# Round three of a graph network: finishing tiles inside the loop of sums, marks by five blocks, an entry that follows the gathers by groups

## The chip, the cores and the metric

The kernel runs on one core of a Trainium2 chip, as one program. The metric is the device time of one execution in microseconds (us). A core has five engines that work side by side, each through its own list of instructions: TensorE (PE, matrix products and transposes; its weight loads are listed as PEld), VectorE (DVE), ScalarE (ACT), GpSimd (POOL, here mostly gathers by index) and SyncE (SP, which only starts transfers). An engine takes its instructions strictly in order: one that waits holds up all that stand behind it.

## The reference, cut to what matters

The network has four rounds. Each adds to the state x (3125 nodes, 256 features, f32) the result of a graph step and then that of a feed-forward step, both on the normalised state:

```
x = x + L2_gnn(layernorm(x), edge_index, edge_weight, ...)   # round three
x = x + L2_ffn(layernorm(x), ...)

def L2_gnn(h, ...):
    deg  = segment_sum(weights with loops, row);  dinv = where(deg > 0, rsqrt(deg), 0)
    norm = dinv[row] * weight * dinv[col]
    xw   = h @ W
    h7   = segment_sum(xw[col] * norm, row) + b
    return relu(h7 @ W1 + b1) @ W2 + b2

def L2_ffn(x, ...):                       # experts gated by graph attention
    h = (x @ W_gat);  a_src, a_dst = sums of h * att_src, h * att_dst
    e = leaky_relu(a_src[src] + a_dst[dst]);  softmax of e over the edges of each dst
    agg = segment_sum(softmax * h[src]);  scores -> two best of four experts -> MLPs
```

Round three's attention runs over edges of its own (65,536 and loops), which the kernel has to bring into the order of their destinations first.

## The kernel before, in words

Nodes lie in T = 25 tiles of P = 128; five tiles are a group (TG = 5). The state X stays in on-chip memory as 128 x 25 x 256. DC = 2 is the number of 128-wide pieces of the 256 features. The edges of the attention lie in 25 blocks, one for each tile, of KB = 17 columns of 128 edges (KL = 8 in the last block).

**Entry.** The experts of round two leave their results in memory (ff_results). `gated` ends with a loop over tiles, `mix_result` (L1018): two gathers by index (gb_y, L348) on POOL's queue and two additions to X on DVE (L1024) for each tile, 50 gathers in all. Round three's `r2_gnn` (L1056) normalises X (`moe_input`, `norm_group` L171: group operations on DVE, a square on ACT, `rsqrt` L153), transposes it (`transposed` L198), and multiplies it by W (r_p, L1080). The scaled result is r2_xw.

**Loop of sums.** `src_sum` (L2379) runs 27 steps. Step t loads one column of the dense graph matrix from memory (ss_wt, 1.6 MB, on SP's queue, L2402, two buffers) and adds up 25 products into ss_sum (L2405, 50 matmul instructions in the trace): the sums of tile t. Beside it, `own_order` (L1839) brings block after block of the attention's edges into order. It is a generator, cut into pieces by `yield`, and the loop takes it a piece at a time:

1. ACT: one-hot matrix oo_h of the block's destinations (17 x L1849, then L1850).
2. DVE: partial sums of it and a scan (L1858 to L1870).
3. PE: two matmuls into oo_p (L1874, L1875). DVE: from them each edge's place (L1879 to L1897, ends in oo_pf). ACT: a second one-hot matrix oo_hp from oo_pf (17 x L1849, L1850). DVE: oo_rh (L1907).
4. PE: 17 matmuls of oo_hp and oo_rh (L1912), which move the edges to their places.
5. DVE: the results are stored in own_gi and own_rel (L1915 to L1917).

A step t takes piece 1 of block t, piece 3 of block t-1, piece 4 of block t-2, the sums of tile t, piece 5 of block t-2, then `done` for tile t-1 (r_acc: two DVE operations, L1086 and L1087), and piece 2 of block t. `in_order` (L1968) makes the order of instructions on PE, DVE and ACT the order in which the program issues them here. So on PE: L1874 and L1875 of block t-1, 17 x L1912 of block t-2, sums of tile t.

**Behind the loop.** `own_marks` (L1920) and `mark_edges` (L1676) find for all 25 blocks where an edge's destination differs from its neighbour's (matmuls of om_ends with om_near, L1939), and turn this into rows of masks: 25 transposes of 4 columns (te_e into te_pr, L1696) and four of 104 columns (L1701), which SP stores as relT. Then r_acc is transposed (L205), the MLP follows in groups of four tiles (L1104, relu L1106, L1111; X += b2 and X += product on DVE, L1113 and L1114), and `r2_ffn` (L2412) begins: loads of expert weights issued by ACT (L2429 to L2433), layernorm, transposes to q_xT, products with the attention weights (100 matmuls, L2454), a copy to q_hx (ACT, L2456), its store to memory (q_rows, SP), and q_ad (DVE, L2458). `attend_blocks` then gathers rows of q_rows for every edge column (ad_rows, L348, 416 gathers on POOL).

The function that the changed kernel calls from step to step is new; of the old ones these lines carry most of the time:

```
            for k in range(kb):                                   # one_hot: ACT, pieces 1 and 3
                nc.scalar.activation(y[:, k, :], self.iotab, AF.Abs, bias=minus[:, k:k + 1])
            nc.scalar.activation(out[:, :kb, :], y[:, :kb, :], AF.Relu, scale=-1.0, bias=self.ones[:, 0:1])
```

Of the kernel before, what the change touches and what calls it, by code (L numbers as in the profile page):

```python
# [24 lines left out]
F32 = mybir.dt.float32  # L25
BF16 = mybir.dt.bfloat16
I32 = mybir.dt.int32
AF = mybir.ActivationFunctionType
OP = mybir.AluOpType
AX = mybir.AxisListType  # L30
PSUM = bass.MemoryType.PSUM
DRAM = bass.MemoryType.DRAM

P = 128
N = 3125
T = 25
NP = T * P
D = 256
DC = D // P
EPS = 1e-5  # L40
BIG = 1e30
NOWHERE = float((1 << 23) + (1 << 22))
GR = 4
TG = 5
# [5 lines left out]
KB = 17  # L50
KL = 8
# [10 lines left out]
class Net:  # L62
# [90 lines left out]
    def rsqrt(self, pool, out, v):  # L153

        nc = self.nc
        r = pool.tile(list(v.shape), F32, name="rs_r")
        h = pool.tile(list(v.shape), F32, name="rs_h")
        nc.scalar.activation(r, v, AF.Sqrt)
        nc.vector.reciprocal(r, r)
        nc.vector.tensor_mul(h, r, r)  # L160
        nc.vector.tensor_mul(h, h, v)
        nc.vector.tensor_scalar(h, h, -0.5, 1.5, op0=OP.mult, op1=OP.add)
        nc.vector.tensor_mul(out, r, h)
# [1040 lines left out]
class Fast(Net):  # L1204
# [471 lines left out]
    def mark_edges(self, s, first, pool, p2, psp):  # L1676

        nc, K = self.nc, s.K
        nc.vector.tensor_scalar(s.neg, s.rel, float(P), -BIG, op0=OP.is_ge, op1=OP.mult)

        go = pool.tile([P, K], F32, name="te_go")
        nc.vector.memset(go, 1.0)
        for k in s.k0:
            nc.vector.memset(go[:, k:k + 1], 0.0)
        st = pool.tile([P, K], F32, name="te_st")
        nc.vector.tensor_tensor_scan(st, go, first, 0.0, OP.mult, OP.max)
        nc.vector.tensor_scalar_mul(s.cum, st, -BIG)
        nc.vector.tensor_scalar(go, go, -1.0, 1.0, op0=OP.mult, op1=OP.add)
        nc.vector.tensor_max(go, go, first)
        nc.vector.tensor_scalar_mul(s.drop, go, -BIG)  # L1690
        for b in range(T):
            e = p2.tile([P, 4], F32, name="te_e")
            k = s.k0[b] + s.kb[b] - 1
            nc.vector.tensor_copy(e, s.cum[:, k:k + 1].to_broadcast([P, 4]))
            ps = psp.tile([P, P], F32, name="te_pr")[0:4, :]
            nc.tensor.transpose(ps, e, self.ident)  # L1696
            nc.vector.tensor_copy(s.dropT[:, b, :], ps)
        W = 104
        for k in range(0, K, W):
            ps = psp.tile([P, P], F32, name="te_pr")[0:W, :]  # L1700
            nc.tensor.transpose(ps, s.rel[:, k:k + W], self.ident)  # L1701
            r = p2.tile([W, P], BF16, name="te_r")
            nc.vector.tensor_copy(r, ps)
            nc.sync.dma_start(s.relT[k:k + W, :], r)
# [90 lines left out]
    def own_load(self):  # L1795
# [6 lines left out]
        self.edge_tiles(s, keep, "own", self.d.rec.rearrange("p k f -> p (k f)"))  # L1802
        s.low = keep.tile([P, KB, KB], BF16, name="own_low")
# [116 lines left out]
    def own_marks(self):  # L1920

        nc, tc, s = self.nc, self.tc, self.o
        K = s.K
        with tc.tile_pool(name="om", bufs=1) as pool, tc.tile_pool(name="om2", bufs=2) as p2, \
                tc.tile_pool(name="om_ps", bufs=2, space=PSUM) as psp:
            n = KB * (T - 1)
            ends = pool.tile([P, 2, T], F32, name="om_ends")
            full = s.rel1[:, 0:n].rearrange("p (d k) -> p d k", k=KB)
            for i, (u, v) in enumerate(((KB - 1, KL - 1), (0, 0))):
                nc.vector.tensor_copy(ends[:, i, 0:T - 1], full[:, :, u])  # L1930
                nc.vector.tensor_copy(ends[:, i, T - 1:T], s.rel1[:, n + v:n + v + 1])
            near = pool.tile([P, 2, P], F32, name="om_near")
            nc.vector.memset(near, 0.0)
            nc.vector.tensor_copy(near[:, 0, 1:P], self.ident[:, 0:P - 1])
            nc.vector.tensor_copy(near[:, 1, 0:P - 1], self.ident[:, 1:P])
            first = pool.tile([P, K], F32, name="om_first")
            ps = psp.tile([P, 2, T], F32, name="om_p")
            for i in range(2):
                nc.tensor.matmul(ps[:, i, :], near[:, i, :], ends[:, i, :], start=True, stop=True)  # L1939
            r, f, l = s.rel1, first, s.last  # L1940
            nc.vector.tensor_tensor(f[:, 1:K], r[:, 1:K], r[:, 0:K - 1], OP.not_equal)
            nc.vector.tensor_tensor(l[:, 0:K - 1], r[:, 0:K - 1], r[:, 1:K], OP.not_equal)
            nc.vector.tensor_tensor(f[:, 0:n].rearrange("p (d k) -> p d k", k=KB)[:, :, 0], full[:, :, 0], ps[:, 0, 0:T - 1], OP.not_equal)
            nc.vector.tensor_tensor(l[:, 0:n].rearrange("p (d k) -> p d k", k=KB)[:, :, KB - 1], full[:, :, KB - 1],
                                    ps[:, 1, 0:T - 1], OP.not_equal)
            nc.vector.tensor_tensor(f[:, n:n + 1], r[:, n:n + 1], ps[:, 0, T - 1:T], OP.not_equal)
            nc.vector.tensor_tensor(l[:, K - 1:K], r[:, K - 1:K], ps[:, 1, T - 1:T], OP.not_equal)
            no = pool.tile([P, K], F32, name="om_no")
            nc.vector.tensor_scalar(no, r, 0.0, 256.0, op0=OP.is_equal, op1=OP.mult)
            nc.vector.scalar_tensor_tensor(s.rel, r, -1.0, no, op0=OP.add, op1=OP.add)  # L1950
            self.mark_edges(s, first, pool, p2, psp)
# [409 lines left out]
    def r1_ffn(self):  # L2361
        with self.mix_way:
            self.gated(self.mix, "L1_ffn_w1", "L1_ffn_b1", "L1_ffn_w2", "L1_ffn_b2", AF.Gelu, send=3)
        self.own_send()
# [14 lines left out]
    def src_sum(self, rows, done):  # L2379


        nc, tc = self.nc, self.tc
        self.own_load()
        with tc.tile_pool(name="ss_w", bufs=2) as wp, tc.tile_pool(name="ss_ps", bufs=2, space=PSUM) as psp, \
                tc.tile_pool(name="oo", bufs=2) as op, tc.tile_pool(name="oo1", bufs=1) as o1, \
                tc.tile_pool(name="oo_ps", bufs=1, space=PSUM) as osp, \
                self.in_order(nc.tensor, nc.vector, nc.scalar):
            ways, sums = {}, {}

            def step(b):  # L2390
                if b in ways:
                    next(ways[b])

            for t in range(T + 2):
                if t < T:
                    ways[t] = self.own_order(t, op, o1, osp)
                step(t)
                step(t - 1)
                step(t - 2)
                if t < T:  # L2400
                    wt = wp.tile([P, T, P], F32, name="ss_wt")
                    nc.sync.dma_start(wt, self.mats[:, t, :, :])  # L2402
                    sums[t] = psp.tile([P, D], F32, name="ss_sum")
                    for d in range(T):
                        nc.tensor.matmul(sums[t], wt[:, d, :], rows[:, d, :], start=d == 0, stop=d == T - 1)  # L2405
                step(t - 2)
                if t - 1 in sums:
                    done(t - 1, sums[t - 1])
                step(t)
        self.own_marks()  # L2410

    def r2_ffn(self):  # L2412
# [7 lines left out]
        with ExitStack() as ctx:  # L2420
            pool = ctx.enter_context(tc.tile_pool(name="q", bufs=1))
# [17 lines left out]
            for e in range(1, E):  # L2439
                nc.vector.memset(early[:, e, 0:e], 1.0)  # L2440
            we = self.head_weights(pool, a["L2_ffn_W_gat"], a["L2_ffn_att_src"].rearrange("h c -> (h c)"),
                                   a["L2_ffn_att_dst"].rearrange("h c -> (h c)"), C=4)
            xT = self.moe_input(pool)
            hx = pool.tile([P, T, Q + 4], F32, name="q_hx")
            ad = pool.tile([P, T, 4], F32, name="q_ad")
            sf = pool.tile([P, T, 4], F32, name="q_sf")
            rows = self.dram.tile([NP, Q + 4], F32, name="q_rows")
            with tc.tile_pool(name="q_ps", bufs=2, space=PSUM) as psp:
                for g in range(0, T, TG):
                    gs = slice(g, g + TG)  # L2450
                    ps = psp.tile([P, TG, Q + 8], F32, name="q_hp")
                    for t in range(TG):
                        for c in range(DC):
                            nc.tensor.matmul(ps[:, t, :], xT[:, c, (g + t) * P:(g + t + 1) * P], we[:, c, :],  # L2454
                                             start=c == 0, stop=c == DC - 1)
                    nc.scalar.copy(hx[:, gs, :], ps[:, :, 0:Q + 4])  # L2456
                    nc.sync.dma_start(rows[g * P:(g + TG) * P, :].rearrange("(t p) w -> p t w", p=P), hx[:, gs, :])
                    nc.vector.tensor_copy(ad[:, gs, :], ps[:, :, Q + 4:Q + 8])  # L2458
                nc.vector.tensor_add(sf, hx[:, :, Q:Q + 4], ad)
                nc.vector.scalar_tensor_tensor(sf, sf, 0.2, sf, op0=OP.mult, op1=OP.max)  # L2460
# [156 lines left out]
```

## Time and profile before

| what | us |
|---|---|
| median of 14 runs | 5074.15 (5064.08 to 5081.76) |
| profiled execution | 5076.92 |
| its span | 5075.1 |
| result gathers of round two, first to last start | 2520.57 to 2583.79 |
| first transpose of round three's entry on PE | 2590.83 |
| first sums in the loop | 2651.94 |
| last sums end | 3011.2 |
| marks, last transpose | 3039.96 |
| transposes of r_acc, first start | 3042.24 |
| MLP, first and last start on PE | 3058.88, 3104.98 |
| layernorm's first square on ACT | 3119.53 |
| score matmuls, start | 3153.48 |

The page of the whole span gives PE 69% busy, DVE 57%, ACT 41%, POOL 41%; the mean granted clock of PE is 0.83 of its full rate. These shares are means over some ten stages with different limits, so the stage that the change touches, from 2520 to 3180, has to be read by itself: which engine is full in it, and what each engine waits for. Rows of the timeline give start, length, engine, line, operation, result and operands, shape and count, and in brackets how long the engine had been idle before and which instruction let it go on. Rows of a stretch give its length and then for each engine the busy time and the number of instructions, then the granted PE clock, the busy share of the DMA engines and GB/s. PE's rows overlap by a little, since matmuls are pipelined.

### The profile page before, as it was taken

To read this page: it belongs to the slowest core of one execution; us is meant where nothing else is said; L and a number is where in the kernel's file an instruction comes from. 1 tells how busy PE (TensorE), PEld (TensorE's weight loads), DVE (VectorE), ACT (ScalarE), POOL (GpSimd) and SP (SyncE) were. 2 spreads that over 40 slices of the span, in tenths; PEclk is the share of its full clock that TensorE was granted. 3 is DMA by queue.
4 is the path that set the end of the run, shared out by engine and by line. 5 is a ranking of instruction groups with operands and counts; after the bars stand their busy time and mean duration, and the time that the engine had idled before them with its cause. 6 is when DMAs were issued, how large, how long until landed. Compare 5 with 4: busy or idle time off the path is not lost. (4 is left out here: it accounts for less than half of the span.)

```text
span 5075.1 us, 65672 instructions
## 1 busy us (share of the span) xinstructions
PE 3490.4 (69%) x20836; PEld 2764.9 (54%) x20836; DVE 2893.3 (57%) x9538; ACT 2062.0 (41%) x5659; POOL 2094.3 (41%) x2082
## 2 busy tenths in 40 slices
PE   1399969646566254553748877057877999988993
PEld 1289958534444143342537754034544788877883
DVE  7988852356665366663358884477765874321112
ACT  3466432136666367661129972022322331112220
POOL 0686443557775777775520000777710000110003
PEclk9699979877777677776969986577887999998997
DMA  1642237544443344432723311111100112215554
GB/s 56 197 138 103 92 119 221 174 117 143 139 143 101 100 137 129 132 105 91 210 68 117 117 71 45 31 35 31 35 5 7 71 66 77 92 68 181 189 191 137
DMA packets 329438, 542.96 MB, mean 107 GB/s; under 512 B 69074, under 2 KB 242006, under 8 KB 325876
## 3 DMA queue, kind: packets, MB, share of 16 engines
q1 hardware_dynamic: 213434, 354.48, 20.7%
q0 software_dynamic: 84032, 154.27, 11.7%
q10 hardware_dynamic: 31610, 29.84, 1.7%
q8 instruction: 172, 2.82, 0.2%
q14 instruction: 190, 1.56, 0.1%
HBM read 393.49 MB, written 145.37 MB: 106 GB/s over the span
## 5 line engine op out<-in xcount | busy, mean ns | idle before, releaser
L348 POOL DMA_INDIRECT ad_rows<-r_rows,fa_gi x832 | 821.6, 988 | 285.0 <-issue 240.2
L1785 POOL DMA_INDIRECT os_table<-os_rec,os_at x512 | 555.6, 1085 | 565.2 <-ACT gx_h L994 171.5
L348 POOL DMA_INDIRECT ad_rows<-q_rows,own_gi x416 | 403.7, 970 | 718.4 <-issue 711.3
L2165 ACT ACTIVATE ad_rows<-ad_rows 128x64 f32<-128x64 f32 x2544 | 617.0, 334 | 1.6
L2175 PE MATMUL ad_acc<-ad_rows,ad_hd 128*128 128x260 f32 x1664 | 518.7, 465 | 4.0 <-ACT ad_rows L2165 2.6
L857 POOL DMA_INDIRECT regions<-gh_xn,gd_at x150 | 157.9, 1053 | 846.5 <-PE r_o L1644 625.5
L1629 PE MATMUL r_pa<-r_xs,r_cnt 128*128 128x257 bf16 x3750 | 468.1, 277 | 28.1 <-DVE r_xs L1405 14.2
L994 ACT ACTIVATE gx_h<-gx_pa,gx_bias 128x256 f32<-128x256 f32 x392 | 185.8, 474 | 586.3 <-PE gx_pa L993 562.2
L1629 PEld LDWEIGHTS <-r_cnt 128*128 128x128 bf16 x3750 | 365.3, 99 | 85.1 <-issue 29.4
L2175 PEld LDWEIGHTS ad_acc<-ad_rows,ad_hd 128*128 128x128 f32 x1664 | 367.3, 233 | 71.1 <-ACT ad_rows L2165 7.1
L2078 PE MATMUL ad_pt<-ident,ad_e 128*4 128x128 f32 x75 | 26.6, 354 | 540.1 <-DVE ad_e L2075 409.6
L965 DVE TENSOR_TENSOR gx_ys<-gx_po,gx_b 128x256 f32<-128x256 f32 x168 | 70.5, 423 | 539.0 <-PE gx_po L963 536.9
L993 PE MATMUL gx_pa<-gx_xt,gx_w 128*128 128x256 f32 x1568 | 367.1, 389 | 4.8 <-DMA gx_w<-in_L_ffn_W 3.4
L963 PE MATMUL gx_po<-gx_w,gx_h 128*128 128x256 f32 x1568 | 366.8, 380 | 0.0
L348 POOL DMA_INDIRECT gb_y<-ff_results,gd_at x150 | 151.1, 1008 | 480.7 <-SPq L120 427.9
L993 PEld LDWEIGHTS gx_pa<-gx_xt,gx_w 128*128 128x128 f32 x1568 | 294.6, 193 | 70.8 <-DVE gx_xt L988 18.7
L2078 PEld LDWEIGHTS ad_pt<-ident,ad_e 128*4 128x4 f32 x75 | 6.1, 82 | 572.6 <-issue 541.5
L963 PEld LDWEIGHTS gx_po<-gx_w,gx_h 128*128 128x128 f32 x1568 | 289.8, 190 | 38.4 <-ACT gx_h L994 2.1
L1510 PE MATMUL r_pa<-r_xn,r_wt 128*128 128x257 f32 x1250 | 300.3, 385 | 9.2 <-ACT r_wt L1545 7.9
L2405 PE MATMUL ss_sum<-r_xw,ss_wt 128*128 128x256 f32 x1250 | 293.9, 398 | 6.3 <-DMA ss_wt<-mats 6.3
L2405 PEld LDWEIGHTS ss_sum<-r_xw,ss_wt 128*128 128x128 f32 x1250 | 248.1, 200 | 43.0 <-issue 6.6
L1510 PEld LDWEIGHTS r_pa<-r_xn,r_wt 128*128 128x128 f32 x1250 | 229.9, 193 | 38.0 <-ACT r_wt L1545 8.5
(556 smaller groups left out, 6911.0 us busy)
## 6 DMA issues: line engine op xcount, KB each, us to landing
gx_w<-in_L_ffn_W SPq DMA_DIRECT2D x56, 1024.0 KB
mats<-r_wt SPq DMA_DIRECT2D x25, 1600.0 KB
ss_wt<-mats SPq DMA_DIRECT2D x25, 1600.0 KB
gx_w<-in_L_ffn_W SPq DMA_DIRECT2D x56, 512.0 KB
regions<-zero SPq DMA_DIRECT2D x26, 1024.0 KB
ad_rb<-fa_relT SPq DMA_DIRECT2D x48, 544.0 KB
gx_xs<-regions SPq DMA_DIRECT2D x84, 256.0 KB
ff_results<-gx_ys ACTq DMA_DIRECT2D x84, 256.0 KB
```

The lines of the kernel that those rows point to most:

```text
L348: return self.nc.gpsimd.indirect_dma_start(out=out, out_offset=None, in_=table[:, :], in_offset=bass.IndirectOffsetOnAxis(ap=idx, axis=0))
L857: ins = nc.gpsimd.indirect_dma_start(out=self.regions[:, :], out_offset=bass.IndirectOffsetOnAxis(ap=m.at[i][:, t:t + 1], axis=0), in_=x, ...
L963: nc.tensor.matmul(po, h[:, f, j * P:(j + 1) * P], w2s[:, f, :], start=f == 0, stop=f == FC - 1)
L965: nc.vector.tensor_add(y[:, j, :], po, b2s)
L993: nc.tensor.matmul(ps, w1s[:, c, f * P:(f + 1) * P], xt[:, c, :], start=c == 0, stop=c == DC - 1)
L994: done = nc.scalar.activation(h[:, f, :], ps, act, bias=bias1[:, f, k:k + 1])
L1510: nc.tensor.matmul(pa, wt[:, i, :], xn[:, g * G + i, :], start=i == 0, stop=i == G - 1)
L1629: nc.tensor.matmul(pa, c[:, u, :], xs[i - 1][:, u, j, :], start=u == 0 and j == 0, stop=u == T - 1 and j == 2)
L1785: i = nc.gpsimd.indirect_dma_start(out=s.table[:, :], out_offset=bass.IndirectOffsetOnAxis(ap=s.at[:, c:c + 1], axis=0), in_=s.rec[:, c, : ...
L2165: i = nc.scalar.activation(v, v, AF.Copy, scale=x.rt[:, k, W4 + h:W4 + h + 1])
L2175: nc.tensor.matmul(x.acc, lhs[:, k, :], rhs[:, k, :], start=i == 0, stop=i == x.kb - 1)
L2405: nc.tensor.matmul(sums[t], wt[:, d, :], rows[:, d, :], start=d == 0, stop=d == T - 1)
```

## The change

It rewrites `r2_gnn` and takes `src_sum` into it; the parts that moved out of `r2_ffn` are gone there.

- **Entry.** The tail of `gated` is left out (`tail=False`); `r2_gnn` itself goes over the five groups: the ten gathers and additions of a group, its layernorm, its transposes (copies all on ACT), its products with W. The 25 additions of b2 to X stand on POOL, issued after the loop of groups; in POOL's own order 15 of them lie between gathers, the first after the 23rd gather, and 10 behind the last.
- **Finish.** `finish(t, total)` is a generator of four pieces for one tile: r_acc's two operations (here lt_acc); transposes (pt) and a copy on ACT; the first product (ph) and two relus on ACT; the second product (po) and the addition to X on DVE. The first is taken at the end of step t+1, the others by `on()`, one in each later step.
- **Scores.** When the last tile of a group is finished, `scores(g)` is added: layernorm of the group, transposes, copies to q_xT, products, store of q_rows, one piece a step, in nine pieces.
- **Marks.** `own_marks` takes five blocks, in two pieces, after the blocks 4, 9, 14, 19 and 24.
- **Order.** `on()` stands behind piece 4 of block t-2 and ahead of the sums of tile t. It takes one piece of everything in the list `later`. After step 26 the rest is taken by repeated `on()`.
- **Buffers.** pt, ph and the score transposes share lt_pt, two buffers of PSUM; po and the score products share lt_po, one buffer; the marks' matmul and transposes share te_pr, one buffer.

```diff
+            near = pool.tile([P, 2, P], F32, name="om_near")
...
+                for g in range(0, T, TG):
+
+                    for t in range(g, g + TG):
+                        self.mix_result(self.mix, bp, t)
+                    xn = xp.tile([P, TG, D], F32, name="r2_xn")
+                    self.norm_group(lp, xn, g)
...
+                for t in range(T):
+                    nc.gpsimd.tensor_add(self.X[:, t, :], self.X[:, t, :], b2)
...
+                    tc.tile_pool(name="om_ps", bufs=1, space=PSUM) as mps, \
...
+                    tc.tile_pool(name="lt_ps", bufs=2, space=PSUM) as bank, \
+                    tc.tile_pool(name="lt_po", bufs=1, space=PSUM) as one, \
+                    self.in_order(nc.tensor, nc.vector, nc.scalar):
...
+                def finish(t, total):
+
+                    acc = tp.tile([P, D], F32, name="lt_acc")
+                    nc.vector.tensor_add(acc, total, xw[:, t, :])
+                    nc.vector.scalar_tensor_tensor(acc, acc, dv[:, t:t + 1], b, op0=OP.mult, op1=OP.add)
+                    yield
+                    pt = bank.tile([P, 512], F32, name="lt_pt")[:, 0:DC * P].rearrange("p (c n) -> p c n", c=DC)
+                    for c in range(DC):
+                        nc.tensor.transpose(pt[:, c, :], acc[:, c * P:(c + 1) * P], self.ident)
+                    at = tp.tile([P, DC, P], F32, name="lt_at")
+                    nc.scalar.copy(at, pt)
+                    yield
+                    ph = bank.tile([P, 512], F32, name="lt_pt")[:, 0:DC * P].rearrange("p (c n) -> p c n", c=DC)
...
+                    for f in range(DC):
+                        nc.scalar.activation(h[:, f, :], ph[:, f, :], AF.Relu, bias=b1[:, f:f + 1])
+                    yield
+                    po = one.tile([P, D], F32, name="lt_po")
+                    for f in range(DC):
+                        nc.tensor.matmul(po, h[:, f, :], w2[:, f, :], start=f == 0, stop=f == DC - 1)
+                    nc.vector.tensor_add(self.X[:, t, :], self.X[:, t, :], po)
+                    if t % TG == TG - 1:
+                        later.append(scores(t + 1 - TG))
...
+                    for u, v in ((0, 2), (2, 4), (4, 5)):
+                        pt = bank.tile([P, 512], F32, name="lt_pt").rearrange("p (c t n) -> p c t n", t=2, c=DC)
...
+                        nc.scalar.copy(q.xT[:, :, (g + u) * P:(g + v) * P].rearrange("p c (t n) -> p c t n", n=P), pt[:, :, 0:v - u, :])
+                        yield
+                    ps = one.tile([P, D], F32, name="lt_po")[:, 0:TG * (Q + 8)].rearrange("p (t w) -> p t w", t=TG)
...
+                    nc.scalar.copy(q.hx[:, gs, :], ps[:, :, 0:Q + 4])
+                    nc.sync.dma_start(q.rows[g * P:(g + TG) * P, :].rearrange("(t p) w -> p t w", p=P), q.hx[:, gs, :])
+                    nc.vector.tensor_copy(q.ad[:, gs, :], ps[:, :, Q + 4:Q + 8])
...
+                def on():
+                    for way in later[:]:
+                        if next(way, StopIteration) is StopIteration:
+                            later.remove(way)
+
                 for t in range(T + 2):
                     if t < T:
                         ways[t] = self.own_order(t, op, o1, osp)
                     step(t)
                     step(t - 1)
                     step(t - 2)
+                    on()
                     if t < T:
                         wt = wp.tile([P, T, P], F32, name="ss_wt")
                         nc.sync.dma_start(wt, self.mats[:, t, :, :])
                         sums[t] = psp.tile([P, D], F32, name="ss_sum")
                         for d in range(T):
+                            nc.tensor.matmul(sums[t], wt[:, d, :], xw[:, d, :], start=d == 0, stop=d == T - 1)
                     step(t - 2)
                     if t - 1 in sums:
-                        done(t - 1, sums[t - 1])
+                        way = finish(t - 1, sums[t - 1])
+                        next(way)
+                        later.append(way)
                     step(t)
+                    if t >= 2 and (t - 2) % TG == TG - 1:
+                        later.append(self.own_marks(mp, mp2, mps, near, t - 1 - TG, t - 1))
+                while later:
+                    on()
```

## The prediction

> **What bounds it now.** First the page's chain that ended last, then busy time by stretch, then the engines' rows inside the stretches that the change touches.
>
> ```profile
> issue 1%; DMA 0%; POOL 0%; DVE 0%; POOLq 0%; DVEq 0%
> ...
> 2660.00:2960.00 300.00, 256.70 (x1425) 218.57 (x1424) 244.91 (x521) 284.04 (x716) 0.00 (x0) 0.95 0.31 114
> 3042.00:3153.00 111.00, 75.69 (x256) 45.43 (x256) 55.81 (x124) 25.20 (x49) 0.00 (x0) 0.70 0.15 44
> 3180.00:3700.00 520.00, 303.91 (x1984) 193.56 (x1984) 359.34 (x1645) 111.75 (x173) 395.60 (x409) 0.75 0.17 33
> ```
> The chain covers 1% of the span, so it says nothing here. In the stretches (PE, PEld, DVE, ACT, POOL) the loop of sums is ACT's: 284 of 300 us. From 3042 to 3153 (transposes, MLP, layernorm) no engine is full. Attention from 3180 on is POOL's: 409 gathers at 0.97 us with 0.30 us between them fill the 520. It starts with
>
> ```profile
> 3176.56 0.94 POOL L348 DMA_INDIRECT ad_rows<-q_rows,own_gi  x1 [591.82 <-issue]
> ```
> so whatever moves the last score store moves the end by as much, one for one. That is my reason to sum everything up to this gather: entry, loop, tail. One step of the loop, on PE, DVE and ACT:
>
> ```profile
> 2797.11 12.72 PE L2405 MATMUL ss_sum<-r_xw,ss_wt 128*128 128x256 f32 x50
> 2809.67 0.22 PE L1874 MATMUL oo_p<-oo_ls,own_oneb 128*128 128x128 bf16 x1
> 2809.73 0.22 PE L1875 MATMUL oo_p<-oo_sm,own_befb 128*128 128x128 bf16 x1
> 2811.14 0.62 PE L1912 MATMUL oo_p<-oo_rh,oo_hp 128*128 128x51 bf16 x17 [1.19 <-ACT oo_hp L1850]
> 2811.61 11.04 PE L2405 MATMUL ss_sum<-r_xw,ss_wt 128*128 128x256 f32 x50
> ...
> 2809.99 1.22 DVE L1879 TENSOR_TENSOR oo_m<-oo_h,oo_p 128x1024 f32<-128x1024 bf16 x1 [3.46 <-PE oo_p L1875]
> 2817.12 0.18 DVE L1897 TENSOR_SCALAR oo_pf<-oo_pi 128x17 f32<-128x17 int32 x1
> ...
> 2811.12 5.07 ACT L1849 ACTIVATE oo_y<-iotab,own_rel 128x128 bf16<-128x128 bf16 x17
> 2816.22 2.11 ACT L1850 ACTIVATE oo_h<-oo_y,ones 128x2176 bf16<-128x2176 bf16 x1
> 2818.36 5.08 ACT L1849 ACTIVATE oo_y<-iotab,oo_pf 128x128 bf16<-128x128 bf16 x17
> ```
> Call P the end of L1875 of a step. DVE turns its result into oo_pf by P+7.3; ACT can then make oo_hp (5.08 + 2.11 us). PE does not wait for this: the next sums start at 2811.61, 14 us before that oo_hp is ready (2818.36 + 7.2). This slack is what the loop lives on; a step is ACT's 5.07 + 2.11 + 5.08 + 2.11 = 14.4. Sums start at 2651.94, sums(24) ends at 3011.2, so the loop takes 359.3 = 25 x 14.4, and the stretch from there to the gather 165.4.
>
> **Removed: the tail.** Transposes of all tiles (3042–3058), the MLP (to 3106), layernorm, transposes and 100 score matmuls
>
> ```profile
> 3153.48 19.40 PE L2454 MATMUL q_hp<-hw_w,xT 128*128 128x24 f32 x100 [0.56 <-issue]
> ```
> go into the loop. After sums(24) there remain: the last block's order, 9.6 us (3011.1 to the last own_rel at 3020.75); finish(24), about 6 (two additions 0.9, transposes 0.69, copy 0.37, four L1104 0.6, two relus 0.75, L1111 0.5, addition 0.4, handovers); the last marks, 8 (31 us for all 25 blocks now, a fifth plus fixed operations); scores(20), 20 (four group operations of DVE at 1.48, square 1.27, six small 0.18, ten transposes 3.0, copies 1.8, ten score matmuls 1.9, handovers 5); the store 3.4 (3172.92 + 0.24 to 3176.56). That is 47. The weight loads that ACT issues take ACT 14.2 in before:
>
> ```profile
> 3119.53 2.43 ACT L186 ACTIVATE ln_sq<-xn 128x1280 f32<-128x1280 f32 x2 [14.21 <-DMA q_b<-in_L_ffn_b]
> ```
> and now stand between the score copies. I count them: 61. Bounds: 50 if they hide behind the marks on DVE, 70 if scores(15) lags too. Tail: -104 (-115 to -95).
>
> **Moved: the entry.** Normalisation, transposes and r_p follow the gathers by groups. What is left behind the last gather (2584.7): its addition to 2587.1; one group's layernorm, about 10; five tiles of transposes, copy, r_p and scaling at 1.7, 8.5; the first load of ss_wt, 6.3 as now. But X += b2 goes to POOL, and 15 of 25 stand between gathers in POOL's order. No such row exists: nearest from below DVE's L1113, same shape, 0.41; from above twice POOL's 128x128 select (0.887), 1.8. I take 0.9, the middle of work on POOL of this size: 13 us, so sums start at 2626 instead of 2651.9: -26 (-33 at 0.41; -12 at 1.8). Behind the gathers' last addition everything of this stage queues, so nothing covers it. The attention weights' load and their product on DVE also move here from behind the MLP (load issued 3106, used 3113.1), ahead of DVE's first addition; the experts' last chunks cover them, so nothing; without that cover the ten gb_y buffers fill and POOL stands for up to those 7 us.
>
> **Added: finish, scores and marks inside the loop.** Their busy time per step: ACT 0.37 + 2 x 0.37, and every fifth step 3.5 for square, copies and root; PE 0.6 + 0.83 + 0.5. A plain step then is ACT's 14.4 + 1.1 = 15.5, PE's about the same to 16.6; 16 taken. The waits cost more. In PE's program order on() stands ahead of sums(t); in ACT's, on()'s pieces stand behind oo_hp(t-1). So any PE piece of on() that needs an ACT or late DVE piece of the same step makes sums(t), and L1875 behind it, wait for P+14.7. Next step's DVE and ACT then wait for that L1875, and the slack shown above is gone. By the changed program's order this happens in:
> - three users of the two lt_pt buffers (score transposes, ph, pt; steps 13, 14, 15, 18, 19, 20, 23, 24): the third waits for the q_xT copy. P+14.7, copy 0.69 (L1106's 128x512), two transposes and handovers 0.8: sums at 16.2, they take 13.7 cold (below), L1875 0.3: 30 each, 8 x 30 = 240.
> - the score matmuls ahead of po (one lt_po buffer; 16, 21): ten matmuls 1.9 and the q_hx copy behind oo_hp, then q_ad's on DVE, then po 0.5 and ph, pt 1.4: sums at P+18, 32 each, 64.
> - marks, first part (7, 12, 17, 22): the neighbour matmul needs the ends, which stand behind DVE's piece up to P+9.1; 0.8 of copies, 1.0 of matmul (L1939), sums 13: 24 each, 96.
> - marks, second part, alone in step 8: DVE's 3.2 of mark operations behind P+9.1 (3022.07 to 3025.22 now), then three transposes of blocks and columns in one te_pr buffer, each with DVE's copy between, 3.0: sums at P+15.3, 29. In 13, 18, 23 it lies under the ACT wait.
> - ten plain steps at 16: 160.
>
> Sum 589 against 359.3: +230. The SP queue gains relT and q_rows stores between the ss_wt loads; each is ready before the next load has to start (a load needs 6.3 of a step), so nothing, and 6.3 for each that comes late.
>
> PE's clock after a wait, granted clock in the sixth number behind the length:
>
> ```profile
> 2652.00:2654.00 2.00, 2.00 (x5) 1.64 (x6) 0.00 (x0) 0.00 (x0) 0.00 (x0) 0.50 1.02 410
> 2658.00:2660.00 2.00, 2.00 (x11) 1.77 (x10) 0.00 (x0) 0.00 (x0) 0.00 (x0) 1.00 0.00 0
> ...
> 2680.96 12.72 PE L2405 MATMUL ss_sum<-r_xw,ss_wt 128*128 128x256 f32 x50
> ```
> After 6.26 us of idleness the first sums began at 0.50 and took 13.7 instead of 11.0; after two waits of 1.6 and 2.0, 12.7. The waits here are 9 to 15 us, so 13.7; with warm sums the eleven longest steps lose 2.7 less and the four of the marks about 1, 34 in all (589 to 555), the low bound. The Trainium skill ("TensorE: Matmul & The Clock Gate", the section on the HAM clock gate) says that one idle window of about 3.4 us halves the clock and about 3.4 us of work restores it. By its figures a cold start loses 1.7 us, an estimate that would make 589 into some 574; it speaks against putting waits ahead of the sums.
>
> **Sum.** +230 - 104 - 26 = +100. On the profiled execution's 5076.9 (span 5075.1, 1.8 around it; median of 14 runs 5074.15) that is 5177; on the median 5174. Bounds: +196 - 115 - 33 = +48 (5122); +265 - 95 - 12 = +158 (5232), where 265 has plain steps at 16.6, 6.3 for a late load in each of three steps and a copy more in the stalled ones.
>
> **Rivals.**
> A. The waits don't bite: each engine works through its queue and a step is the busiest engine's, PE 12.2 + 2.95 + 1.3 + 0.4 = 16.9, 25 x 17 = 425, +66 - 104 - 26 = -64: 5010. For it: the two-step lead in the order. Against it: the same-step needs above. It decides the sign below an average step of (359.3 + 130)/25 = 19.6.
> B. They bite, but the sums stay warm: 555, +196 - 130 = +66: 5140. For it: the short transposes ahead of the sums. Against: the 0.50 row.
> C. A late wait on SP too: a store of relT or q_rows ahead of a load, 6.3 in ten steps, +63 more: 5237. For it: the store needs DVE or ACT of the stalled step. Against: two ss_wt buffers.
> D. Stalled steps cost about 19 to 20 on average, and gain and loss cancel: 5074.
>
> **How the numbers follow.** The forecast 0.53, B 0.20, C 0.10, A 0.14, D 0.03. A measurement of this kernel tells about 0.2% (10 us) from no change. Faster 0.15, same 0.03, slower 0.82. The likeliest case's own range is 5122 to 5232; for 8 in 10 it goes down through B's lower half to 5085 and up to C, 5235; A and D stay out.
>
> **What would show it.** In the loop, PE rows of L2566 with 9 to 15 us of idleness just ahead of the on() piece, released by ACT's q_xT or DVE, in the named steps, and PE's clock 0.5 behind them; plain steps of 16; sums(24) ending near 3215; first ad_rows gather about 61 later; sums starting near 2626, POOL additions of about 0.9. Wrong it is if sums follow without such waits (A), if POOL additions cost several us, or if the first gather does not set the end.

## The result and the profile after

The changed kernel takes 5138.93 us (median of 6 runs, 5131.9 to 5144.91) against 5073.99 for the kernel before (28 runs): a ratio of 1.0129, 95% interval 1.0119 to 1.0138, or 65 us more. Its profiled execution took 5136.13, its span is 5134.1.

The timeline of PE in the changed kernel: three plain steps, then step 12 (marks, first part), step 14 (three users of lt_pt) and step 16 (score products). The columns are as before: start, length, engine, line, operation, count, and in brackets the idle time and its releaser. Rows between those shown are left out.

```profile
2685.05 10.96 PE L2566 MATMUL ss_sum<-r_xw,ss_wt 128*128 128x256 f32 x50
2697.66 0.62 PE L1931 MATMUL oo_p<-oo_rh,oo_hp 128*128 128x51 bf16 x17 [1.54 <-ACT oo_hp L1869]
2700.18 10.96 PE L2566 MATMUL ss_sum<-r_xw,ss_wt 128*128 128x256 f32 x50
2715.31 10.96 PE L2566 MATMUL ss_sum<-r_xw,ss_wt 128*128 128x256 f32 x50
...
2835.95 1.02 PE L1956 MATMUL te_pr<-om_ends,om_near 128*128 128x5 f32 x4 [8.24 <-DVE om_ends L1950]
...
2878.48 0.22 PE L1894 MATMUL oo_p<-oo_sm,own_befb 128*128 128x128 bf16 x1
2880.33 1.05 PE L2495 MATMUL lt_pt<-lt_at,r_W 128*128 128x128 f32 x8
2893.87 0.69 PE L2487 MATMUL lt_pt<-ident,lt_acc 128*128 128x128 f32 x2 [12.49 <-ACT q_xT L2536]
2894.35 13.70 PE L2566 MATMUL ss_sum<-r_xw,ss_wt 128*128 128x256 f32 x50
...
2951.49 2.07 PE L2501 MATMUL lt_po<-r_W,lt_h 128*128 128x256 f32 x4 [12.36 <-DVE q_ad L2545]
```

and ACT's in step 14:

```profile
2886.13 5.07 ACT L1868 ACTIVATE oo_y<-iotab,oo_pf 128x128 bf16<-128x128 bf16 x17 [12.29 <-DVE oo_pf L1916]
2891.24 2.11 ACT L1869 ACTIVATE oo_hp<-oo_y,ones 128x2176 bf16<-128x2176 bf16 x1
2893.25 0.56 ACT L2536 COPY q_xT<-lt_pt 128x512 f32<-128x512 f32 x1
```

Plain steps follow each other at 15.1 us. In step 14 the two transposes of L2487 stand in front of the sums and wait 12.49 us for the q_xT copy, which stands in ACT's list behind oo_hp; oo_hp waits for oo_pf, and that follows L1894 (P = 2878.7; q_xT's copy ends at P + 15.1). Before, nothing in front of the sums needed this step's oo_hp. The busy time by stretch shows the same, first for steps 3 to 7 (four plain ones and one with marks), then from step 13's sums to step 24's (length, then busy time of PE, PEld, DVE, ACT, POOL, granted clock, DMA share, GB/s); the last two rows are the clock behind the wait of step 14:

```profile
2660.00:2736.86 76.86, 63.93 (x397) 56.00 (x396) 62.72 (x139) 76.34 (x198) 0.00 (x0) 0.97 0.29 108
2865.63:3177.38 311.75, 184.30 (x998) 157.97 (x998) 160.96 (x380) 168.41 (x434) 0.00 (x0) 0.77 0.15 54
2896.00:2898.00 2.00, 2.00 (x6) 1.58 (x5) 0.00 (x0) 2.00 (x8) 0.00 (x0) 0.50 0.00 0
2900.00:2902.00 2.00, 2.00 (x11) 1.77 (x10) 0.00 (x0) 2.00 (x1) 0.00 (x0) 1.00 0.00 0
```

In the first ACT is full. In the second no engine is busy for more than 60% of the time: the engines wait for one another in turn.

The stage in three pieces, from the profiles of the two kernels:

| piece | before | after | difference |
|---|---|---|---|
| first result gather to first sums | 2520.57 to 2651.94: 131.4 | 2510.40 to 2624.86: 114.5 | -16.9 |
| loop, first sums to end of sums(24) | 359.3 | 2624.86 to 3191.46: 566.6 | +207.3 |
| tail, to the first ad_rows gather | 165.3 | to 3240.65: 49.2 | -116.1 |
| sum | 656.0 | 730.3 | +74.3 |

The span differs by 59.0: the first gather starts 10.2 earlier in this profile, and from the first ad_rows gather to the end it is 1893.5 instead of 1898.5. Both lie outside what the change touches; the first gather's start spreads from 2509.6 to 2520.6 over the six profiles on such chips.

### The profile page after: what moved, and what is told of

Its sections match the earlier page's. It is cut to its first block, busy times and chain, and to the rows that moved or that the text cites. A ratio compares the mean times of both kernels' runs of the same rounds, so it can differ in the third digit from the quotient of the medians.

```text
span 5134.1 us, 66025 instructions
## 1 busy us (share of the span) xinstructions
PE 3494.2 (68%) x20997; PEld 2793.3 (54%) x20997; DVE 2879.0 (56%) x9469; ACT 2072.1 (40%) x5723; POOL 2115.4 (41%) x2107
## 3 DMA queue, kind: packets, MB, share of 16 engines
q0 software_dynamic: 84032, 154.27, 11.5%
## 5 line engine op out<-in xcount | busy, mean ns | idle before, releaser
L1634 PE MATMUL r_pa<-r_xs,r_cnt 128*128 128x257 bf16 x3750 | 467.7, 277 | 28.1 <-DVE r_xs L1410 14.2
L1634 PEld LDWEIGHTS <-r_cnt 128*128 128x128 bf16 x3750 | 365.1, 99 | 84.8 <-issue 29.4
L2566 PE MATMUL ss_sum<-r_xw,ss_wt 128*128 128x256 f32 x1250 | 306.3, 410 | 6.6 <-DMA ss_wt<-mats 6.6
L2566 PEld LDWEIGHTS ss_sum<-r_xw,ss_wt 128*128 128x128 f32 x1250 | 259.4, 210 | 47.3 <-issue 7.0
```

The source lines that it names most:

```text
L1634: nc.tensor.matmul(pa, c[:, u, :], xs[i - 1][:, u, j, :], start=u == 0 and j == 0, stop=u == T - 1 and j == 2)
L2566: nc.tensor.matmul(sums[t], wt[:, d, :], xw[:, d, :], start=d == 0, stop=d == T - 1)
```

## The experiments

Theory: PE's pieces of on() that need an ACT or DVE result of the same step hold the sums behind them. Rivals: the added work is too long for a step; the clock; the entry's or the tail's own costs. The runs came to four chips. On two of them, those of the first eight runs, the kernel before takes 5802 to 5804 us; the gathers by index of the attention (ad_rows) run at a slower pace there (numbers in the last section). On the other two, those of the last four runs, it takes 5072 to 5077. All differences are to the kernel before on the same chip. The loop, which has no such gathers, can be compared across chips. Gather times are those of the 50 result gathers, from the first start to the last: 63 us before, 80 in the changed kernel, both on a chip of the faster kind; the kernel before has no profile on a slower chip.

**The changed kernel again.**

> The changed kernel once more, beside the kernel before on the chip of the runs below, since the first four experiments ran on a chip on which the kernel before takes 5804 us. The loop of sums does not gather by index, so its length in the profile should be 566 again, and the difference to the kernel before +65 (58 to 75) on any chip. If the difference is much larger on a chip with slow gathers, part of it lies outside the loop and the tail.

5869.36 against 5801.91: +67.5, ratio 1.0122 (1.0103 to 1.0141); the loop takes 567. The loss is the same on a slower chip.

**The same work, behind the sums.**

```diff
                     step(t - 2)
-                    on()
                     if t < T:
                         wt = wp.tile([P, T, P], F32, name="ss_wt")
...
                         next(way)
-                        later.append(way)
                     step(t)
+                    on()
+                    if t - 1 in sums:
+                        later.append(way)
```

> The changed kernel with on() taken at the end of each step, behind the sums of tile t and behind piece 2 of block t; the work and the buffers are the same. Theory (the loss is that PE waits inside on() ahead of the sums): sums follow the last step's L1893/L1894 and L1931 at once and run while ACT makes oo_hp; what is left of a wait is P + 14.7 against the sums' end at P + 11.6, so steps of 16.5 with three users of lt_pt, 16.5 with the marks' first part, 18.5 with the score products, 21 with the marks' second part: 10 x 15.2 + 4 x 16.5 + 21 + 5 x 16.5 + 3 x 21 + 2 x 18.5 = 422 against 566; the tail is some 4 longer, as one on() more lies behind the last sums. 5139 - 145 + 4 = 4998 (4975 to 5030). Rival (the work itself is too much for the step): no more than 20 us better, as the same instructions run on the same engines.

5716.82 against 5803.79: -87.0, ratio 0.9847 (0.9823 to 0.9872), so 154 better than the changed kernel with its +67.5. The loop takes 405 where 422 was expected, the tail 54. PE of a step with three users of lt_pt:

```profile
3349.43 11.04 PE L2565 MATMUL ss_sum<-r_xw,ss_wt 128*128 128x256 f32 x50
3360.31 0.60 PE L2535 MATMUL lt_pt<-ident,lt_xn 128*128 128x128 f32 x4
3361.61 1.05 PE L2495 MATMUL lt_pt<-lt_at,r_W 128*128 128x128 f32 x8
3364.32 0.44 PE L2487 MATMUL lt_pt<-ident,lt_acc 128*128 128x128 f32 x2 [1.66 <-ACT q_xT L2536]
3365.16 2.19 PE L2565 MATMUL ss_sum<-r_xw,ss_wt 128*128 128x256 f32 x9
```

The wait of 12.49 is now 1.66, because the 11.04 us of sums run while ACT makes oo_hp, and they run warm. No instruction was taken away, so the length of the added work is not what made the kernel slower.

**Another buffer for the score transposes.**

```diff
-                        pt = bank.tile([P, 512], F32, name="lt_pt").rearrange("p (c t n) -> p c t n", t=2, c=DC)
+                        pt = mps.tile([P, 4 * P], F32, name="te_pr").rearrange("p (c t n) -> p c t n", t=2, c=DC)
```

> The changed kernel, with the score transposes written into the marks' PSUM buffer (te_pr) instead of lt_pt, so that ph and pt have the two lt_pt buffers to themselves. Theory (the wait for the q_xT copy behind oo_hp is a wait for a buffer): steps 14, 15, 19, 20 and 24 fall from 28 to 29 us to plain ones of 15.2, 5 x 13.3 = 66 less; in steps 13, 18 and 23 the marks' own transposes now stand behind the q_xT copy, 4 us more each, 12. Net -54: 5085 (5070 to 5100). Rival (the steps are long because the added work is long, or because PE's clock is low): the same steps stay near 28 and the time stays at 5139.

5818.44 against 5803.79: +14.6, ratio 1.0026 (1.0014 to 1.0038), 53 less than the changed kernel's +67.5. Steps 14, 15, 19, 20 and 24 take 14.8 to 15.6; 13, 18 and 23 rise to 31.4 to 32.1. The wait went with the buffer, and where the marks now share it, it came back at the place that was named. (Steps 16 and 21, which were not in the account, rise too, from 31.4 to 33.7.) A third lt_pt buffer was not tried.

**The copies on DVE.** on() stays in front of the sums.

```diff
-                        nc.scalar.copy(q.xT[:, :, (g + u) * P:(g + v) * P].rearrange("p c (t n) -> p c t n", n=P), pt[:, :, 0:v - u, :])
+                        nc.vector.tensor_copy(q.xT[:, :, (g + u) * P:(g + v) * P].rearrange("p c (t n) -> p c t n", n=P), pt[:, :, 0:v - u, :])
...
-                    nc.scalar.copy(q.hx[:, gs, :], ps[:, :, 0:Q + 4])
+                    nc.vector.tensor_copy(q.hx[:, gs, :], ps[:, :, 0:Q + 4])
```

> The changed kernel with on() where it was, ahead of the sums, but the copies to q_xT and q_hx on DVE instead of ACT. Theory (the length of the wait is set by what stands ahead of the copy on its engine): on ACT it is oo_hp, ready at P + 14.7; on DVE it is piece 3, done at P + 9.1, so PE's wait of 12.5 falls to about 7: steps 14, 15, 19, 20 and 24 from 28.5 to 23, the two with score products from 31.4 to 26; 13, 18 and 23 stay, since the marks hold them on DVE. 5 x 5.5 + 2 x 5 = 38 less: +27 against the kernel before (+15 to +40). Rival (it is the missing third buffer as such, or the clock, that makes the step long): +65.

5830.67 against 5801.91: +28.8, ratio 1.0058 (1.0041 to 1.0075). PE in step 15:

```profile
3403.76 1.05 PE L2495 MATMUL lt_pt<-lt_at,r_W 128*128 128x128 f32 x8
3411.90 0.69 PE L2487 MATMUL lt_pt<-ident,lt_acc 128*128 128x128 f32 x2 [7.08 <-DVE q_xT L2536]
3412.38 13.31 PE L2566 MATMUL ss_sum<-r_xw,ss_wt 128*128 128x256 f32 x50
```

7.08 instead of 12.49, with the same two buffers: the price of the wait is what stands in front of the copy on its engine, piece 3 of DVE instead of oo_hp of ACT. Steps 14, 15, 19, 20 and 24 take 22.7 to 23.1 (23 expected), the two with score products 26.9 and 27.0 (26). The sums behind these waits still run cold (12.3 to 13.4), so these 39 us come from the waits and not from the clock.

**The entry alone**, in the kernel before (tail=False, the loop over groups as in the change, X += b2 left on DVE behind the loop):

> The kernel before with the new entry alone: gathers, layernorm, transposes and r_p by groups; loop, marks, MLP and scores stay behind as they were, X += b2 stays on DVE behind the loop. Theory: the result gathers take 64 us as before (no POOL additions between them), and from the last gather to the first sums 34 us pass instead of 67, as in the changed kernel: 5074 - 33 = 5041 (5030 to 5052). Rival (the entry's gain is only the 17 us that the changed kernel shows between the first gather and the first sums, and the rest of its earlier start comes from before the stage): 5057.

5779.85 against 5803.79: -23.9, ratio 0.9961 (0.9946 to 0.9977). This lies between the two numbers, and neither reason was right: the gathers took 73 us, where 64 were expected from a faster chip's profile, and 41 us instead of 34 passed behind them. The next experiment shows a pause in the midst of the gathers.

**b2 on DVE, no additions on POOL.**

```diff
-                for t in range(T):
-                    nc.gpsimd.tensor_add(self.X[:, t, :], self.X[:, t, :], b2)
...
                     nc.vector.scalar_tensor_tensor(acc, acc, dv[:, t:t + 1], b, op0=OP.mult, op1=OP.add)
+                    nc.vector.tensor_add(self.X[:, t, :], self.X[:, t, :], b2)
```

> The changed kernel without the 25 additions on POOL; X += b2 is done on DVE in the first piece of finish, 0.41 us in each step. Theory: 15 additions of 0.8 no longer stand between the gathers, and the gathers no longer lengthen beside them: 80.7 us of gathers become 64 to 65, DVE has room in the loop: 5139 - 16 = 5123 (5115 to 5130). Rival (the gathers wait for something else, for DVE or for their data): 5139.

5868.12 against 5803.79: +64.3, ratio 1.0109 (1.0088 to 1.0131), 3 less than the changed kernel. The gathers take 74 us instead of 78 on such a chip, and DVE stands still in their midst for 12 us, ACT for most of them:

```profile
3058.96 0.48 DVE L1029 SCALAR_TENSOR_TENSOR X<-gb_y,gd_w,X 128x256 f32<-128x256 f32 x1
3071.61 0.48 DVE L2458 TENSOR_SCALAR r_xw<-r_p,r_dv 128x256 f32<-128x256 f32 x1 [12.17 <-remote]
...
3065.35 0.37 ACT L2454 COPY r_xt<-r_pt 128x256 f32<-128x256 f32 x1 [4.51 <-remote]
```

"remote" is what the profile shows where it finds no instruction of the program that let the engine go on. The kernel with the entry alone pauses at the same place of its entry.

**q_hx on DVE, with on() behind the sums.**

> on() at the end of the step (as in e2_on_last), and the copy to q_hx moved from ACT to DVE. Theory: in the two steps with score products po waits for q_ad behind q_hx behind oo_hp on ACT, 4.0 us in e2_on_last's profile; on DVE the copy follows the matmuls at once: 21.5 becomes some 17, two steps, 9 less; the tail gains 1 or 2. Against the kernel before: -87 in e2_on_last, here -97 (-90 to -105). Rival: another user of lt_po or DVE's order holds these steps, and they stay at 21.5: -87.

5712.56 against 5801.91: -89.3, ratio 0.9853 (0.9834 to 0.9872). The two steps fall from 21.3 and 21.6 to 17.3 and 17.9 and the loop to 394.7, as expected. The whole time missed the range (-90 to -105) and is not told apart from -87.0, since the intervals overlap: in the two profiles the stage is 11.7 shorter, but its first gather starts 11.5 later, and nothing in this run shows why.

**That, and no additions on POOL.**

> e6_last_hx without POOL's additions of b2 (DVE does them in finish, as in e5_b2_dve). In e5_b2_dve the gathers without additions took 74 us, not 64, since DVE, ACT and PE all stood for some 12 us in the middle of the entry with no releaser of this program shown. If that pause belongs to this order of the entry (it comes whenever POOL's additions are gone), first gather to first sums is 112 again and the time is 3 below e6_last_hx: -100. If it was a chance of those two profiles, the gathers take 64 to 66 and the time is 14 below: -111.

5704.44 against 5801.91: -97.5, ratio 0.9843 (0.9826 to 0.986); gathers of 75 us, with pauses of DVE of 8.27 and 4.00 us by "remote". So the pause came in each of the three kernels without the additions on these two chips, one profile of each.

**Additions with unused results.** The same kernel with POOL adding X and b2 into a tile that nothing reads.

> e7_last_hx_b2 with 25 additions X + b2 on POOL put back between the gathers, their result left unused (X gets b2 on DVE in the loop as in e7_last_hx_b2): POOL's breaks between the gathers are there again, and nothing else of the entry changes. If the 12 us pause of DVE, ACT and PE comes with gathers that follow each other without a break, it is gone here, the gathers take 78 to 80 us with the additions among them, first gather to first sums is 114 to 116 and the time against the kernel before is -90 to -97. If the pause has to do with the order of instructions on the other engines, it stays, the gathers take some 88, and the time is 10 to 14 longer than e7_last_hx_b2: -85.

4977.22 against 5072.45, on a chip with fast gathers: -95.2, ratio 0.9813 (0.9798 to 0.9828). Gathers of 81 us, first gather to first sums 115.8, no pause. By itself this tells nothing, as the next run on the same chip has no pause either.

**lt_at on DVE**: q_hx and b2 on DVE, no additions on POOL, and `nc.vector.tensor_copy(at, pt)` instead of `nc.scalar.copy(at, pt)`.

> e7_last_hx_b2 with the copy to lt_at on DVE instead of ACT. Theory: plain steps are ACT's (14.4 + 0.37 + 0.7 = 15.4, measured 15.1), so taking 0.37 away from ACT makes them 14.8, while DVE, which waits for PE in every step, has room: 20 steps by 0.3 = 6 less, and pt's copy no longer stands behind oo_hp: -104 against the kernel before. Rival: DVE's order (piece 3, then the rest) makes the copy late, and the steps get longer: -90.

4974.16 against 5072.45: -98.3, ratio 0.9812 (0.9799 to 0.9826). The gathers take 68 and no engine pauses, though POOL has no additions: first gather to first sums 100.9. Plain steps are 14.9 instead of 15.1, as expected, but the loop takes 405.0, 7 more than the same kernel with this copy on ACT took on a slower chip. On the fourth chip that kernel's loop takes 404.3 too (last run below), so the move shows neither gain nor loss in the loop.

**Two kernels again, on the fourth chip, whose gathers are fast too.** First the changed kernel without POOL's additions:

> e5_b2_dve once more (the changed kernel without POOL's additions). On the chip with slow gathers it was only 3 below the changed kernel, as DVE, ACT and PE paused for 12 us; in e10_at_dve, on a chip where the kernel before takes 5072, the pause was absent and the gathers took 68. If the pause belongs to the chip and this is the other one, first gather to first sums is 100 to 102 instead of 115 and the difference to the kernel before is +65 - 14 = +51 (+45 to +56): the forecast's price of the additions holds. If the pause belongs to the kernels without additions, it is +62 to +65 on any chip.

5129.7 against 5077.27: +52.4, ratio 1.0104 (1.0087 to 1.0121). Gathers 67, first gather to first sums 101.0 against 114.5, no pause. So POOL's additions cost 13 us on such a chip. On the two chips with slow gathers a pause of about the same size took their place; its cause is open.

Then the candidate for the best version, on() behind the sums with q_hx and b2 on DVE:

> e7_last_hx_b2 once more: on() at the end of the step, q_hx on DVE, b2 on DVE; the candidate for the best version. Its loop took 397.5 in the profile, e10_at_dve's 404.5, at the same entry. Against the kernel before: -98 - 7 = -105 (-100 to -110) on the chip with fast gathers and without the pause; -97 with it.

4971.3 against 5077.27: -106.0, ratio 0.9791 (0.9775 to 0.9808). This version beats both kernels. Its stage is 101.0 + 404.3 + 51.0 = 556 against 656.

## Why the prediction came out as it did

The sign and the mechanism were right; the time lies 35 below the forecast and inside its range. In the profiles the stage is 26 below it: 23 in the loop and 12 in the tail, less 9 that the entry gained too little. The remaining 9 lie outside the stage, where the forecast expected no change; no run here explains them.

- **Which steps wait, and for what.** As forecast, to the step: the third user of lt_pt for q_xT behind oo_hp (14, 15, 19, 20, 24; in 13, 18 and 23 most of the wait is the marks' te_e, and q_xT ends it), po for q_ad (16, 21), the marks for om_ends (7, 12, 17, 22) and te_e (8). Moving on() (154 us), moving the buffer (53 us) and moving the copies (39 us) each took away what this account says.
- **Their sizes.** Marks' first part 21.6 to 24.9 (24), second 28.7 (29), score products 31.4 and 31.3 (32): right. Three users 28.0 to 29.4 (30) and plain steps 15.1 (16) were a little high, and the loop grew by 207 instead of 230. P + 14.7 was right; the cold sums were priced too high.
- **The clock.** Sums behind a long wait were priced at 13.7, by one row. Of the 15 sums behind a long wait one ran warm (step 16, behind 3.5 us of other matmuls); the other 14 take 11.87 to 14.00, mean 12.95, against 10.96 warm: 2.0 each is lost, not 2.7. The Trainium skill ("TensorE: Matmul & The Clock Gate", the section on the HAM clock gate) says that the clock is halved after an idle window of about 3.4 us and restored after as much work. By its figures a cold start loses 1.7, an estimate; the mean of the trace lies between that and the row, nearer to the rule. So the clock accounts for 14 x 2.0 = 28 of the 207, and the waits and the longer plain steps for the rest.
- **The tail.** What failed here: the 14.2 us that ACT spends on issuing weight loads were counted in full. They lie beside PE's and DVE's work between 3214 and 3229, and the tail takes 49.2, 0.8 below the lower bound that was given for this case. The list of what remains was short, too: scores(10)'s products and all of scores(15) from its layernorm on also lie behind sums(24) (DVE's L2513 at 3197.02, PE's L2541 at 3200.88 and 3220.62). That makes the last block's order end 17.3 behind the sums instead of 9.6; finish(24) then takes 6.1 (6), the marks 5.0 (8), scores(20) 17.4 (20), the store 3.4. So 47 for all but the loads was near by luck, as the misses cancel, and the 70 that was given for a lagging scores(15) did not come: it lags, and the tail is 49.
- **The entry.** -26 was forecast; the first sums do start 27.1 earlier, near the forecast's 2626, but that is luck: 10.2 of it come from before the stage, and the stage itself gives 16.9. The price of the POOL additions (13, at 0.9 each; they take 0.79 on average) was right on such a chip, as the run without them on the fourth chip shows (114.5 - 101.0 from first gather to first sums). What was too low is the rest behind the last gather: two groups' layernorm and transposes stood there, not one (r_xn's transposes start at 2596.56 and 2609.26), 33.7 from the last gather's end to the sums where 27 were counted.
- **The rivals.** A falls: the average step is 22.7, above the 19.6 from which the sign turns. D falls: the 15 stalled steps take 27.7 on average, not 19 to 20. B's number, 5140, is almost the one measured, but its reason, sums that stay warm, is not what happened: the tail and the outside made up for it. C (late loads on SP) does not show: no sums but the first wait for ss_wt.
- **One for one.** The shift of the first ad_rows gather passes to the end, but for 5 us: 64.1 later there, 59.0 at the end.

## What to carry to other kernels

Work that is put into a loop whose order is fixed costs less by its length than by where its operands stand in the other engines' lists: ask of each inserted instruction whether it needs a result of the same step, and, if it does, put it behind the longest block that needs none. Two buffers shared by three users in a step are such a need, too, though no data passes between them. The same pieces behind the sums instead of in front of them made this change 106 us faster than before instead of 65 slower (with one copy, q_hx, and the addition of b2 moved besides; the move behind the sums alone gave 87 on a slower chip).

## What the runs showed of the hardware

Chips differ in the pace of the ad_rows gathers far more than in the loop of sums: the 416 gathers run from first to last start in 527 to 529 us in the six profiles on one kind and in 720 to 727 in the eight on the other, while POOL's median for one is 0.94 to 0.95 us on both. The loop of the same kernel differs by less than 2%, and the 50 result gathers, with POOL's additions among them, take 80 and 81 on the one kind and 77 to 80 on the other. On the two slower chips, and only in the kernels whose gathers were not broken by POOL additions, DVE paused for some 12 us some 43 us behind the first gather, and ACT and PE did little meanwhile; the profile shows no instruction that releases them, and the cause was not found.
